# Layer 0's last norm: half blocks, the mean subtracted by TensorE, Ln and Exp in place of root and reciprocal, norm and gate fused on VectorE

## The chip, the cores and the metric

The kernel runs on one core of a Trainium2 chip, in one launch. The metric is the device time of a run in microseconds (us): the median of three runs of the kernel before is 10,872.56 us (10,855.62 to 10,873.84). All data are float32.

## The reference, cut to what matters

The kernel computes a network of four layers. Layer 0 is a selective scan over four images of 64 x 64 tokens with 256 inner channels, and it ends in a norm over the channels, a gate and a projection back to 128 channels:

```python
y = ys[:, 0]... + ys[:, 1]... + ys[:, 2]... + ys[:, 3]...   # four scan directions
mu = jnp.mean(y, axis=-1, keepdims=True)
var = jnp.mean(jnp.square(y - mu), axis=-1, keepdims=True)
y = (y - mu) * jax.lax.rsqrt(var + LN_EPS) * ln_w + ln_b
y = y * jax.nn.silu(z)
return y @ w_out
```

The result is added to the layer's input, and layer 1 reads the sum. Layers 1 to 3 and their feed-forward parts are not touched by the change.

## The kernel before, in words

**Where the work stands.** `layer0` runs image after image. An image goes through `front` (group norm, input projection), `middle` (convolution, step sizes), the scan, and `back` (the norm above). Channels lie on the 128 partitions, in two halves `h`; tokens lie along the free axis. `back` works on eight blocks of 512 tokens.

**The scan loop** has 512 turns `I`: 4 images x 2 channel halves x 64 chunks of 64 tokens. Turn I of image b is called by its half h and chunk c. Its work comes in two equal parts, kp 0 and kp 1. For each part TensorE makes 32 small products into two PSUM banks (L668; the banks `db` are three), VectorE adds the carry twice (L684) and runs two scans (L687), and GpSimd takes the new carry (L694) and multiplies the states by C in one product of 128 x 2048 elements (L702). Once in a turn, between its two parts, VectorE also multiplies `xo` and `dt` into `du` for the next turn (L644). TensorE sums the states of the turn before last (L722), ScalarE copies these sums out (L736), makes the diagonal tiles of the next turn in half 0 (L636, 16 instructions) and the decay factors (L591).

**What runs beside it.** `front(b + 1)`, `middle(b + 1)` and `back(b - 1)` are generators. The loop takes one step of the running generator at up to three places of a turn:

```python
scan(I, now, 0, bs, st, carry, new)     # two scans
...
    next(beside, None)                  # first place
...
bs = products(now, 1)
if nxt:
    inputs(nxt)                         # L644
scan(I, now, 1, bs, st, carry, new)     # two scans
    next(beside, None)                  # second place
...
if beside and h == 0 and c % 4 == 2:
    next(beside, None)                  # third place
```

So what a step of the first place puts on VectorE stands between the second scan and L644; what a step of the second or third place puts there stands between the fourth scan and the next turn's first. On TensorE, ScalarE and VectorE the order is the written one (`manual_schedule`), and each of them is one queue in order; for GpSimd and for SyncE, which issues the loads and stores, a scheduler sets the order. The order of generators in images 1 and 2 is `back(b - 1)`, `front(b + 1)`, `middle(b + 1)`; in image 3 it is `back(2)` alone; image 0 has other generators there. They begin at chunk 5 of half 0. Whatever is left of them at chunk 59 of half 1 is run at once there, in front of that turn (`if h and c == NCHUNK - QC - 1: for _ in beside: pass`). The beside work has one PSUM bank, `bg`.

`back` has 11 steps a block: loads of `yr`, `zs` and `x` (into tiles `t4k`, four buffers, and `t2k`), a sum of two partial results on GpSimd (L501), the mean over channels by TensorE with a matrix of 1/256 (L508), two subtractions on VectorE (L513), two squares on ScalarE (L517), the variance by TensorE (L521), a root on ScalarE (L523), a reciprocal and two products on VectorE (L525, L527), scale and bias on ScalarE (L530), the product with the gate `zl` on GpSimd (L534), the projection on TensorE (L541), and the residual on VectorE (L545).

**After the loop** the last image's `back(3)` has no loop to run beside. `recurrence_and_attention` runs it beside `prepare(0)`, the first image of layers 1 and 2: one step of `back` for every two of `prepare`, with two banks in turn (`bg`, `blk`). Here a scheduler sets the order on every engine. `prepare(0)` must be done before the attention loop (its first score product is L1431).

Below stand the functions that the diff touches and their callers, with the profile's line numbers.

Of the kernel before, what the change touches and what calls it, by code (L numbers as in the profile page):

```python
# [8 lines left out]
AF = mybir.ActivationFunctionType  # L9
ALU = mybir.AluOpType  # L10
# [4 lines left out]
P = 128  # L15
# [4 lines left out]
D = 128  # L20
BLK = 512
# [3 lines left out]
DI = 256  # L25
# [34 lines left out]
def tl(pool, shape, tag, dtype=F32, bufs=None):  # L60
    return pool.tile(shape, dtype, name=tag, tag=tag, bufs=bufs)
# [99 lines left out]
def layer0(cm, x, W, x1, also, kept):  # L161
# [5 lines left out]
    with ExitStack() as ctx:  # L167
# [30 lines left out]
        nc.vector.tensor_scalar(A, A, -1.0, None, ALU.mult)  # L198
        d4 = tl(wp, [P, 2], "d4")
        nc.vector.tensor_scalar(d4, vec[:, 2, :], 4.0, None, ALU.mult)  # L200
        avg = tl(wl, [P, P], "avg")
        nc.vector.memset(avg, 1.0 / DI)

        mask = tl(wp, [P, QR], "mask")
        for r in range(4):
# [277 lines left out]
        def back(b, bank, tmp=tmp, t4=t4):  # L483


            def fetched(k, *names):
# [2 lines left out]
                    nc.sync.dma_start(t, img[b][name][:, :, k * BLK : (k + 1) * BLK])  # L489
                return ts  # L490

            (y0,) = fetched(0, "y0")
            yield
            for k in range(NBLK):
                cols = slice(k * BLK, (k + 1) * BLK)
                xr = tokens(b, k, tmp)
                y, zl = fetched(k, "yr", "zs")
                yield
                yield
                yield  # L500
                nc.gpsimd.tensor_tensor(y, y, y0, ALU.add)  # L501
                if k + 1 < NBLK:
                    (y0,) = fetched(k + 1, "y0")
                yield
                yield
                ps = bank()
                for h in range(2):
                    nc.tensor.matmul(  # L508
                        ps, lhsT=avg, rhs=y[:, h, :], start=(h == 0), stop=(h == 1)
                    )  # L510
                sq = []
                for h in range(2):
                    nc.vector.tensor_tensor(y[:, h, :], y[:, h, :], ps, ALU.subtract)  # L513
                yield
                for h in range(2):
                    sq.append(tl(tmp, [P, BLK], "t2k"))
# [6 lines left out]
                nc.scalar.activation(sd, ps, AF.Sqrt, bias=cm.eps5[:, 0:1])  # L523
                yield
                nc.vector.reciprocal(ps, sd)  # L525
                for h in range(2):
                    nc.vector.tensor_tensor(y[:, h, :], y[:, h, :], ps, ALU.mult)  # L527
                yield
                for h in range(2):
                    nc.scalar.activation(  # L530
                        y[:, h, :], y[:, h, :], AF.Identity,
                        bias=vec[:, 4, h : h + 1], scale=vec[:, 3, h : h + 1],
                    )
                nc.gpsimd.tensor_tensor(y, y, zl, ALU.mult)  # L534
                yield
                yield
                ps = bank()
                po = ps.rearrange("p (t c) -> p t c", c=D)
                for i in range(4):
                    for h in range(2):  # L540
                        nc.tensor.matmul(  # L541
                            po[:, i, :], lhsT=y[:, h, i * P : (i + 1) * P], rhs=w_out[:, h, :],
                            start=(h == 0), stop=(h == 1),
                        )
                nc.vector.tensor_tensor(xr, xr, po, ALU.add)  # L545
                nc.sync.dma_start(x1[b, cols, :].rearrange("(t p) c -> p t c", p=P), xr)


# [1808 lines left out]
```

## Time and profile before

| | |
|---|---|
| median of three runs | 10,872.56 us |
| the profiled execution's own time | 10,860.27 us |
| its span, first to last instruction | 10,858.5 us |
| VectorE (DVE) busy | 7,823.8 us, 72% of the span |
| TensorE (PE) busy | 8,928.9 us, 82% |
| ScalarE (ACT) busy | 5,313.2 us, 49% |
| GpSimd (POOL) busy | 5,452.4 us, 50% |
| scan loop, first to last scan | 341 to 6,246 us |
| from there to the first score product L1431 | 6,246 to 6,640 us |

The profile is one execution. A group row names the line, the engine, the operation, its output and inputs, their shapes (partitions x elements) and the count; behind the bar stand the time in which at least one of them ran, the mean time of one in ns, and the idle time of the engine just before them with what ended most of it. A matmul in float32 leaves two records. TensorE's records overlap, so that the time of a group, and not its count by its mean, tells how long TensorE was taken.

### The profile page before, as it was taken

Reading aid. Unit: us, or ns where it says so; the run is one execution under the profiler, and the core shown is the slowest. Engines: PE = TensorE matmul, PEld = TensorE weight load, DVE = VectorE, ACT = ScalarE, POOL = GpSimd, SP = SyncE. Lnnn points to the kernel's source line nnn. Section 1 sums busy time; section 2 is a strip of 40 time slices with the busy share of each in tenths; the row PEclk is TensorE's granted clock in tenths of the full one; section 3 lists DMA queues with packets and bytes.
Section 4 is the critical chain, followed back from the end, with each engine's and each line's share of the span. In section 5 each row is a group of like instructions: output and inputs, shape, how many; then the busy total and the mean of one; then the engine's idle time right before and its main releaser. Section 6 shows DMA issues by size and latency. Waiting matters only on the chain. (4 is left out here: it accounts for less than half of the span.)

```text
span 10858.5 us, 190052 instructions
## 1 busy us (share of the span) xinstructions
PE 8928.9 (82%) x72040; PEld 4226.5 (39%) x72040; DVE 7823.8 (72%) x10667; ACT 5313.2 (49%) x13151; POOL 5452.4 (50%) x2661
## 2 busy tenths in 40 slices
PE   6668998779887788887788846999999956998886
PEld 2333443334333333333333323444444434544442
DVE  1799999999999999999999965546361132445546
ACT  5557554556444565445532124767676613333321
POOL 0579999879888888888899920000000000000000
PEclk7789998889888889888888968999999976577767
DMA  5434554335443345443333231111100083012101
GB/s 150 105 91 128 145 140 110 103 98 153 131 119 110 109 117 141 130 119 102 99 94 94 74 117 38 36 35 36 32 27 16 16 226 70 26 37 57 41 20 47
DMA packets 1155618, 960.91 MB, mean 88 GB/s; under 512 B 191940, under 2 KB 905384, under 8 KB 1148312
## 3 DMA queue, kind: packets, MB, share of 16 engines
q1 hardware_dynamic: 1140888, 898.41, 29.2%
q0 software_dynamic: 13824, 50.34, 2.6%
q8 instruction: 579, 9.49, 0.4%
q14 instruction: 327, 2.68, 0.1%
HBM read 616.68 MB, written 331.61 MB: 87 GB/s over the span
## 5 line engine op out<-in xcount | busy, mean ns | idle before, releaser
L687 DVE TENSOR_TENSOR_SCAN big<-dA,db 128x1024 f32<-128x1024 f32 x2048 | 4679.5, 2286 | 81.9 <-PE db L668 3.1
L702 POOL TENSOR_TENSOR big<-big,ct 128x2048 f32<-128x2048 f32 x1024 | 4648.2, 4539 | 78.7 <-DVE big L687 0.2
L668 PE MATMUL db<-dg,du 32*64 32x256 f32 x32768 | 1952.0, 427 | 822.1 <-DVE db L684 674.5
L722 PE MATMUL yp<-big,both 128*64 128x256 f32 x16384 | 2368.9, 438 | 66.2 <-ACT yc L736 58.2
L722 PEld LDWEIGHTS yp<-big,both 128*64 128x64 f32 x16384 | 1250.6, 155 | 1152.0 <-issue 752.8
L668 PEld LDWEIGHTS db<-dg,du 32*64 32x64 f32 x32768 | 672.3, 138 | 2079.6 <-issue 1909.5
L736 ACT COPY yr<-yp 128x64 f32<-128x64 f32 x1024 | 224.4, 220 | 1618.2 <-PE yp L722 1617.8
L1480 PE MATMUL av<-e,x 128*128 128x512 f32 x2048 | 974.0, 592 | 4.6 <-ACT e L1475 4.6
L1431 PE MATMUL qk<-a,xT 128*128 128x512 f32 x2048 | 966.6, 594 | 8.7 <-ACT e L1435 7.9
L1435 ACT ACTIVATE e<-qk,nk 128x512 f32<-128x512 f32 x1024 | 693.3, 685 | 539.5 <-PE qk L1431 538.4
L591 ACT ACTIVATE dA<-dp,A 128x252 f32<-128x252 f32 x2048 | 866.1, 499 | 98.1 <-DVE big L687 48.3
L636 ACT ACTIVATE dg<-mask,BT 128x32 f32<-128x32 f32 x4096 | 898.5, 323 | 5.3 <-PE db L668 5.3
L1010 POOL TENSOR_TENSOR g_rs<-g_rs,qrow 128x4 f32<-128x4 f32 x32 | 41.1, 1285 | 1500.4 <-DVE g_rs L1009 1500.4
L694 POOL TENSOR_TENSOR cy<-big,a 128x32 f32<-128x32 f32 x1008 | 347.4, 345 | 571.3 <-DVE big L687 374.8
L1431 PEld LDWEIGHTS qk<-a,xT 128*128 128x128 f32 x2048 | 378.0, 190 | 462.4 <-issue 358.0
L1480 PEld LDWEIGHTS av<-e,x 128*128 128x128 f32 x2048 | 381.6, 190 | 434.8 <-issue 393.7
L1475 ACT ACTIVATE e<-e 128x1024 f32<-128x1024 f32 x510 | 538.8, 1056 | 15.5
L644 DVE TENSOR_TENSOR du<-xo,dt 128x256 f32<-128x256 f32 x512 | 533.1, 1041 | 12.8 <-DMA xo<-xT_d 12.8
L1956 ACT ACTIVATE e<-s 72x576 f32<-72x576 f32 x448 | 273.3, 643 | 512.2 <-PE s L1949 509.2
L1967 POOL COPY vp<-vt 72x160 f32<-72x160 f32 x56 | 19.6, 352 | 909.6 <-PE po L1973 906.8
L2189 DVE SCALAR_TENSOR_TENSOR tex<-x,gw,tex 128x128 f32<-128x128 f32 x768 | 264.2, 344 | 254.6 <-PE x L2183 239.8
L1913 DVE TENSOR_REDUCE mx<-s 96x6 f32<-96x864 f32 x224 | 226.0, 1047 | 291.0 <-PE s L1905 290.7
(528 smaller groups left out, 9883.4 us busy)
## 6 DMA issues: line engine op xcount, KB each, us to landing
ct<-ct_d SPq DMA_DIRECT2D x1024, 128.0 KB
xo<-xT_d SPq DMA_DIRECT2D x2048, 32.0 KB
dg_d<-dg SPq DMA_DIRECT2D x256, 256.0 KB
dg<-dg_d SPq DMA_DIRECT2D x256, 256.0 KB
t4k<-xc_d SPq DMA_DIRECT2D x384, 132.0 KB
dT_d<-t2k SPq DMA_DIRECT2D x256, 128.0 KB
dp<-dl_d SPq DMA_DIRECT2D x256, 128.0 KB
dt<-dT_d SPq DMA_DIRECT2D x512, 64.0 KB
```

Source lines behind the costliest of these rows:

```text
L591: nc.scalar.activation(w["dA"][:, :, g, n, 1:], w["dp"][:, g, :, 1:], AF.Exp, scale=A[:, w["h"], g, n : n + 1],)
L636: nc.scalar.activation(q["dg"][:, n, :], mask, AF.Copy, scale=BT[:, q["c"], n : n + 1])
L644: nc.vector.tensor_tensor(q["du"], q["xo"], q["dt"].unsqueeze(1).to_broadcast([P, 2, P]), ALU.mult)
L668: nc.tensor.matmul(bs[j][p * TC : (p + 1) * TC, g * NH0 : (g + 1) * NH0, t0 : t0 + QR], lhsT=q["du"][rows, kp, g * TC : (g + 1) * TC], rhs ...
L687: nc.vector.tensor_tensor_scan(st[:, u].rearrange("p n t -> p (n t)"), q["w"]["dA"][:, c % QC].rearrange("p g n t -> p (g n t)"), bs[j].re ...
L694: nc.gpsimd.tensor_tensor(new[:, us, :], st[:, us, :, TC - 1], quads[(I + 1) // QC]["a0"][:, (c + 1) % QC] .rearrange("p g n -> p (g n)"). ...
L702: nc.gpsimd.tensor_tensor(sv, sv, q["ct"].rearrange("p n t -> p (n t)").unsqueeze(1) .to_broadcast([P, 4, NH0 * TC]), ALU.mult,)
L722: nc.tensor.matmul(yp[p * TC : (p + 1) * TC], lhsT=both, rhs=st[:, :, p * NH0 + n, :], start=(n == 0), stop=(n == NH0 - 1),)
L1431: nc.tensor.matmul(ps, lhsT=me["xT"][:, kt * P : (kt + 1) * P], rhs=me["a"][k], start=True, stop=True,)
L1435: nc.scalar.activation(e[:, j, :], ps, AF.Exp, bias=me["nk"][:, kt : kt + 1], scale=2.0)
L1475: nc.scalar.activation(es[g + 2], es[g + 2], AF.Exp)
L1480: nc.tensor.matmul(avs[b, k], lhsT=img[b]["x"][:, kt, :], rhs=e[:, j, :], start=(kt == 0), stop=(kt == NT - 1),)
```

## The change

`back` now works on half blocks of 256 tokens, two for each block. For each:

- TensorE takes y less its mean in one bank, with a matrix `cen` (identity less 1/256) and a matrix `navg` (-1/256): four products of 256 columns. ScalarE copies the result out (`yc`) and squares it (`sq`).
- TensorE makes the negative variance with `navg`; ScalarE takes Ln of the variance plus 1e-5 and Exp of -0.5 times it, into the same bank.
- VectorE has two fused instructions for each channel half: (yc x ln_w) x root into PSUM, and (that + ln_b) x zl into `yc`.
- TensorE projects 256 tokens, and VectorE adds them to the residual.

GpSimd's gate product is gone; its sum y + y0 stays. A block has 12 steps in place of 11.

```diff
-        avg = tl(wl, [P, P], "avg")
-        nc.vector.memset(avg, 1.0 / DI)
+        navg = tl(wl, [P, P], "navg")
+        nc.vector.memset(navg, -1.0 / DI)
+        cen = tl(wl, [P, P], "cen")
+        nc.vector.tensor_tensor(cen, cm.ident, navg, ALU.add)
...
-                yield
-                ps = bank()
-                for h in range(2):
-                    nc.tensor.matmul(
-                        ps, lhsT=avg, rhs=y[:, h, :], start=(h == 0), stop=(h == 1)
-                    )
-                sq = []
-                for h in range(2):
-                    nc.vector.tensor_tensor(y[:, h, :], y[:, h, :], ps, ALU.subtract)
-                yield
-                for h in range(2):
-                    sq.append(tl(tmp, [P, BLK], "t2k"))
-                    nc.scalar.activation(sq[h], y[:, h, :], AF.Square)
-                yield
-                ps = bank()
-                for h in range(2):
-                    nc.tensor.matmul(ps, lhsT=avg, rhs=sq[h], start=(h == 0), stop=(h == 1))
-                sd = tl(tmp, [P, BLK], "t2k")
-                nc.scalar.activation(sd, ps, AF.Sqrt, bias=cm.eps5[:, 0:1])
-                yield
-                nc.vector.reciprocal(ps, sd)
-                for h in range(2):
-                    nc.vector.tensor_tensor(y[:, h, :], y[:, h, :], ps, ALU.mult)
-                yield
-                for h in range(2):
-                    nc.scalar.activation(
-                        y[:, h, :], y[:, h, :], AF.Identity,
-                        bias=vec[:, 4, h : h + 1], scale=vec[:, 3, h : h + 1],
-                    )
-                nc.gpsimd.tensor_tensor(y, y, zl, ALU.mult)
-                yield
-                yield
-                ...
-                nc.vector.tensor_tensor(xr, xr, po, ALU.add)
+                for s in range(2):
+                    part = slice(s * half, (s + 1) * half)
+                    yield
+                    ps = bank().rearrange("p (h t) -> p h t", h=2)
+                    for o in range(2):
+                        for h in range(2):
+                            nc.tensor.matmul(
+                                ps[:, o, :], lhsT=cen if o == h else navg, rhs=y[:, h, part],
+                                start=(h == 0), stop=(h == 1),
+                            )
+                    yc = tl(tmp, [P, 2, half], "t2k")
+                    sq = tl(tmp, [P, 2, half], "t2k")
+                    nc.scalar.copy(yc, ps)
+                    nc.scalar.activation(sq, ps, AF.Square)
+                    yield
+                    ps = bank().rearrange("p (h t) -> p h t", h=2)
+                    for h in range(2):
+                        nc.tensor.matmul(
+                            ps[:, 0, :], lhsT=navg, rhs=sq[:, h, :],
+                            start=(h == 0), stop=(h == 1),
+                        )
+                    nc.scalar.activation(
+                        sq[:, 0, :], ps[:, 0, :], AF.Ln, bias=cm.eps5[:, 0:1], scale=-1.0
+                    )
+                    nc.scalar.activation(ps[:, 0, :], sq[:, 0, :], AF.Exp, scale=-0.5)
+                    yield
+                    for h in range(2):
+                        nc.vector.scalar_tensor_tensor(
+                            ps[:, 1, :], yc[:, h, :], vec[:, 3, h : h + 1], ps[:, 0, :],
+                            ALU.mult, ALU.mult,
+                        )
+                        nc.vector.scalar_tensor_tensor(
+                            yc[:, h, :], ps[:, 1, :], vec[:, 4, h : h + 1], zl[:, h, part],
+                            ALU.add, ALU.mult,
+                        )
+                    yield
+                    ps = bank()
+                    po = ps[:, 0:half].rearrange("p (t c) -> p t c", c=D)
+                    for i in range(2):
+                        for h in range(2):
+                            nc.tensor.matmul(
+                                po[:, i, :], lhsT=yc[:, h, i * P : (i + 1) * P],
+                                rhs=w_out[:, h, :], start=(h == 0), stop=(h == 1),
+                            )
+                    nc.vector.tensor_tensor(
+                        xr[:, 2 * s : 2 * s + 2, :], xr[:, 2 * s : 2 * s + 2, :], po, ALU.add
+                    )
```

More of the change, by code (lines that the diff above doesn't have):

```diff
@@ L490, in fetched @@
                 return ts
+            half = BLK // 2
             (y0,) = fetched(0, "y0")
@@ L529, in back @@
-                for h in range(2):
-                    nc.scalar.activation(
-                        y[:, h, :], y[:, h, :], AF.Identity,
-                        bias=vec[:, 4, h : h + 1], scale=vec[:, 3, h : h + 1],
-                    )
-                nc.gpsimd.tensor_tensor(y, y, zl, ALU.mult)
-                yield
-                yield
-                ps = bank()
-                po = ps.rearrange("p (t c) -> p t c", c=D)
-                for i in range(4):
+                for s in range(2):
[14 more added lines that the diff above has]
+                    ps = bank().rearrange("p (h t) -> p h t", h=2)
@@ L540, in back @@
                     for h in range(2):
                         nc.tensor.matmul(
-                            po[:, i, :], lhsT=y[:, h, i * P : (i + 1) * P], rhs=w_out[:, h, :],
+                            ps[:, 0, :], lhsT=navg, rhs=sq[:, h, :],
                             start=(h == 0), stop=(h == 1),
                         )
-                nc.vector.tensor_tensor(xr, xr, po, ALU.add)
+                    nc.scalar.activation(
+                        sq[:, 0, :], ps[:, 0, :], AF.Ln, bias=cm.eps5[:, 0:1], scale=-1.0
+                    )
```

## The prediction

> **What bounds the kernel now.** First the page, because `back` lives in the scan loop and in the stretch behind it. Its slices (40 of 271 us, busy share in tenths) and two of its groups:
>
> ```profile
> DVE  1799999999999999999999965546361132445546
> POOL 0579999879888888888899920000000000000000
> ...
> L687 DVE TENSOR_TENSOR_SCAN big<-dA,db 128x1024 f32<-128x1024 f32 x2048 | 4679.5, 2286 | 81.9 <-PE db L668 3.1
> L702 POOL TENSOR_TENSOR big<-big,ct 128x2048 f32<-128x2048 f32 x1024 | 4648.2, 4539 | 78.7 <-DVE big L687 0.2
> ```
>
> VectorE is full from 340 to 6,246 us, and GpSimd nearly: a turn has 4 scans of 2.29 on one and 2 products of 4.54 on the other. From the starts of L687 in the timeline, a turn with nothing beside it takes 10.1 to 10.2 us. So inside the loop what is put on VectorE costs its time, or more. Where it costs more, the instructions of `du` show:
>
> ```profile
> L644 DVE TENSOR_TENSOR du<-xo,dt x512: 359/512/4772, 338.2 to 6230.5; 128x256 f32<-128x256 f32 x171
> ```
>
> The same instruction takes 0.36 or 4.77 us. Two answers of the timeline (start, us, engine) say when, in image 3:
>
> ```profile
> 4962.28 0.40 DVE L644 TENSOR_TENSOR du<-xo,dt 128x256 f32<-128x256 f32 x1
> ...
> 5023.73 0.69 DVE L545 TENSOR_TENSOR t2k<-t2k,bg 128x512 f32<-128x512 f32 x1
> 5024.34 4.72 DVE L644 TENSOR_TENSOR du<-xo,dt 128x256 f32<-128x256 f32 x1
> ...
> 5024.26 4.52 POOL L702 TENSOR_TENSOR big<-big,ct 128x2048 f32<-128x2048 f32 x1
> ```
>
> The reader is to see that L644 straight after the scan takes 0.40; behind 0.69 us of beside work it begins 0.08 us after GpSimd's product and ends 0.28 us after it. Both read two SBUF tensors, and one waits for the other. L702 begins 0.42 us (GpSimd idle) to 0.6 us after the scan's end; L644s that began 0.10 us or more ahead of it took at most 0.53 us. So a step of the first place that holds VectorE longer than about 0.4 us costs some 5 us whatever it does, and one of the second place costs its own time. Turns in image 3's `back` bear it out: first place with L545 15.2, with L525/L527 15.2, with L513 15.2 and 15.7 (and 14.3 and 11.6 where GpSimd was late); second place with L545 10.5, with L513 11.2, with L525/L527 14.5.
>
> The work to be replaced, in the loop (24 of 32 blocks):
>
> ```profile
> L525 DVE RECIPROCAL bg<-t2k 128x512 f32<-128x512 f32 x24 | 80.0, 3333 | 0.0
> L534 POOL TENSOR_TENSOR t4k<-t4k 128x1024 f32<-128x1024 f32 x24 | 56.3, 2346 | 10.4 <-ACT t4k L530 10.4
> L448 ACT ACT_TABLE_LOAD x50 | 64.2, 1283 | 0.9
> L523 ACT ACT_TABLE_LOAD x24 | 30.8, 1283 | 0.4
> ```
>
> and the waits behind the loop (6,255 to 6,640 us), where the sum's two waits are the only large ones that `back` brings to VectorE:
>
> ```profile
> DVE t2k L545 <- PE bg L541: 12.5, 3, 6.1
> ...
> DVE t2k L545 <- PE blk L541: 9.3, 3, 6.3
> ```
>
> **The parts.** *VectorE's own time.* Before, a block has 3.34 (L525) + 4 x 0.68 (L513, L527) + 0.68 (L545) = 6.7 us. After, it has 8 fused instructions and 2 additions on 256 columns. The addition: L644 alone, 0.40. The fused one is bounded by 0.41 (L450, the same form on 512 without a pointer, 0.67 less 256 columns at 1.04 ns) and 0.48 (L2063, with a pointer, 0.75, likewise); I take 0.48, the same kind. So a group S of four is 1.9 us, and a block 4.7: 2.0 us less. All have a PSUM operand, and L527, which has one too, stays at 0.67 to 0.69 under GpSimd's products.
>
> *Where they fall.* The order of the two built programs gives each step's place. Per image, before: L525/L527 3 in first places and 5 later, L513 4 and 4, L545 4 and 4. Measured against 10.15 us a turn, the turns of `back` (chunks 7 to 44) cost 102, 100 and 92 us: 98 per image. After, with 4 VectorE steps a block in place of 3: S 7 in first places, 9 later; additions 6 in first places, 10 later. Per image:
>
> - S first: 7 x 4.65 (turns of `middle` with 2.1 us there, L450 to L454, take 14.8) = 32.6. S later: 9 x 1.9 = 17.1.
> - Additions first: 0.40 us leaves L644 about 0.17 us ahead of L702, so no wait: 6 x 0.45 = 2.7; later, 7 x 0.35 = 2.5 (3 more are in the next item).
> - Third places. A TensorE step that needs VectorE's second-place step of its own turn holds back the next products, 1.95 us: `front` shows it, 19.2 us at chunk 46 (three L296) against 15.4 at 45 (two). The projection after S, 3 times: 1.1 (half of L541's 2.2 a block) + 1.95 = 3.1 each, 9.3. The centring after an addition, 3 times: 2.2 (as many columns as L508's 2.1 a block) + 1.95 = 4.2, 12.6.
> - TensorE elsewhere: the centring that waits for the one bank until a first-place addition, 3 x 1.5 = 4.5 (BT's copy L429 in that place costs 1.2 with a shorter product behind it); ten other centrings of 2.2 in a half turn that has some 1.7 to spare: before, L521 of the same size cost 1.0 to 2.5 at chunks 8 and 13; 1.2 each, 12; two variances in third places, 2.4.
> - GpSimd: L534 hid under L525 (turns with it: 10.4 to 10.5), so its going gives nothing. Two of the sums L501 (2.4) now stand in turns without a collision and delay L644: 4.8.
>
> The sum is 100.5, against 98: +7 for three images. VectorE's saving is eaten by one more step in the wrong place and by third-place waits.
>
> At those chunks the granted clock was 0.54 (4,994 to 5,001 us) after TensorE had been idle for 2.07 us. The Trainium skill (TensorE: Matmul & The Clock Gate, Part 1) has the clock fall after an idle window of about 3.4 us; by it those centrings would run at full clock and cost nearer 0.6, 6 us less an image. The row decides.
>
> *ScalarE.* Per half: copy and square 1.2, Ln and Exp 0.8, and tables. L448 is Ln, and the page of the loop shows a load before each one, 1.28 us; the built program has 62 loads for 64 Ln and 64 for 64 Exp at the new lines, against 28 before roots, and 28 fewer elsewhere: 70 more in all, 90 us of ScalarE. In the loop that hides: a turn of half 0 holds 3.5 (L636) + 1.7 (L591) + 0.6 (L736), and `front`'s turns, with two loads and more work, take 10.1.
>
> *`middle` comes 8 steps later.* `back` of images 1 and 2 has 8 more steps, and the steps left at chunk 59 are run in one piece. Before, nothing with VectorE work is left; after, the last block's nine steps are (L429 to L475; in the built order seven VectorE instructions stand behind chunk 58). They form one chain through one bank: w_dt 1.44, ScalarE 4.6 and 5.9 (with one and two loads), VectorE 2.05, for both halves, with an overlap of 0.7 each: 16.5; then 2 x (0.8 + 0.6 + 1.2 + 0.6) + hops = 6.8; less the last copy, plus the products: TensorE can give the next scan its data about 25 us late. In its old places this cost 11.5 (chunks 55 to 58). 2 x 13.5 = +27. `front` keeps its cost, about 27 an image.
>
> *Behind the loop* (8 blocks). Less VectorE time 8 x 2.0 = 16; less collision with L534 (five slow instructions there have 10 us over their usual time, 5.9 under L534) 6; the waits of L545 (21.8) and L513 (3.2) 25: -47. But a half block is now a chain: projection 1.7, centring 2.8, ScalarE 1.2, variance 1.4 (sizes of this stretch, where L541 and L508 are slower), Ln, load, Exp 2.2, hops 0.4: 9.7 us from one S to the next, because the bank is freed by S. In the built order VectorE has 2 to 11 us of other work between them; summed over 15 gaps the lacking time is 45. So -2. The Trainium skill (ScalarE: Activation LUTs, Table sets: the hidden batching unit) says that one set holds Ln and Exp, one load for both; then the chain is 8.4 and the sum some 17 us lower. Loads before each in the built program speak against it; I go by them.
>
> **Sum.** 7 + 27 - 2 = +32 on the profiled execution's 10,860.3 (span 10,858.5 and 1.8 around it): 10,892. The median of runs is 12 us above that execution: 10,905.
>
> **Rivals.** *The lock is missed (faster).* Where GpSimd is late, L644 passes: at chunk 35 of half 1 in image 1, L450 to L454 stood in the first place and the turn took 13.3, L644 0.40. If S (1.9 us) ended ahead of L702, 21 places would cost 2.0 in place of 4.65: -56, 10,849. It needs GpSimd to be 1.5 us behind at that point; the sum L501 does that in few turns, and L534's going makes it rarer. *The chain behind the loop is hidden (no change).* VectorE's other work covers the 45 us: 10,860. It decides at 9.7 us against the 6 us that the built order leaves on average. *The additions meet the lock (much slower).* 0.17 us of margin is small; if they miss it, 18 x 4.2 = +76: 10,981. *The tables are one set:* 10,888 and no further.
>
> **Numbers.** The forecast 0.50, with its own range of 10,870 to 10,945; missed lock 0.17; hidden chain (or a flush that overlaps more) 0.20; additions in the lock 0.13. A measurement of this kernel tells 0.2%, 22 us, from no change. Faster: the missed lock and a little of the hidden chain, 0.18. Same: most of the hidden chain and the low end of the forecast, 0.27. Slower: the rest, 0.55. The range reaches from 10,842 to 10,985.
>
> **What would show it.** L644's spread: about 7 of some 4.7 us in each `back`, under S, and none under the additions; turns at chunks 10, 14, 26, 30, 42, 46 long by third-place waits; a gap of about 25 us at chunk 59 of half 1 in images 1 and 2, and none in image 3; 126 loads at the new lines, 1.28 each; behind the loop S waiting for ScalarE, and L1431 near 390 us after the last scan. The forecast is wrong if the first-place S costs 2 us, if additions cost 5, if chunk 59 stays at 10 us, or if L1431 comes 30 us sooner after the last scan.

## The result, and the profile after

The changed kernel takes 10,947.22 us (median of 6 runs, 10,910.27 to 10,957.58), the kernel before in the same comparison 10,874.51 us (6 runs): a ratio of 1.0057, with a 95% interval of 1.0037 to 1.0076. It is slower by 73 us between the medians, and by 40 to 83 us by the interval. The profiled execution took 10,950.13 us, its span is 10,948.4 us.

The page of the changed kernel, with the rows that answer to those of before. Lines behind `back` have moved by 9: the scan is L696, `du` L653, GpSimd's product L711, the carry's addition L693. The slices are the busy shares in tenths; in a row, busy time and mean of one in ns stand behind the first bar, and the idle time before it with what ended it behind the second.

```profile
DVE  1699999999998999989999956545451132445546
POOL 0579999779878888878899910000000000000000
...
L696 DVE TENSOR_TENSOR_SCAN big<-dA,db 128x1024 f32<-128x1024 f32 x2048 | 4679.3, 2286 | 82.0 <-PE db L677 3.1
L711 POOL TENSOR_TENSOR big<-big,ct 128x2048 f32<-128x2048 f32 x1024 | 4646.1, 4537 | 79.3 <-POOL cy L703 0.4
```

The scans and the products cost what they did. VectorE, full before, now shows slices of 8: it has less to do in the loop and waits more. Its new groups in the changed kernel, and the loads of tables in front of Ln and Exp:

```profile
L535 DVE SCALAR_TENSOR_TENSOR bg<-t2k,vec,bg 128x256 f32<-128x256 f32 x112 | 53.3, 476 | 24.5 <-ACT bg L532 22.7
L539 DVE SCALAR_TENSOR_TENSOR t2k<-bg,vec,t4k 128x256 f32<-128x256 f32 x112 | 54.1, 483 | 3.5
L552 DVE TENSOR_TENSOR t2k<-t2k,bg 128x256 f32<-128x256 f32 x56 | 22.5, 402 | 23.4 <-PE bg L548 23.4
...
L532 ACT ACT_TABLE_LOAD x64 | 82.1, 1283 | 1.2
L529 ACT ACT_TABLE_LOAD x62 | 79.5, 1283 | 35.7 <-PE bg L525 23.7 <-PE blk L525 11.4 <-issue 0.2
```

The instructions cost what the forecast gave them: the fused ones 0.48 us, the additions 0.40. The time must have gone elsewhere. Adding up the turns from the starts of the scans gives where (us; half 1 of image 3 is 653.7 and 653.4):

| | before | after | difference |
|---|---|---|---|
| start to first scan | 341.4 | 349.3 | +7.9 |
| image 0 | 1,443.4 | 1,446.7 | +3.3 |
| half 0 of images 1, 2, 3 (`back`, then `front`) | 2,327.1 | 2,333.9 | +6.8 |
| half 1 of images 1, 2 (`middle`) | 1,479.9 | 1,528.8 | +48.9 |
| last scan to first score product | 394.9 | 408.0 | +13.1 |
| from there to the end | 4,218.1 | 4,228.2 | +10.1 |

The first and the last row hold code that the change doesn't touch; over all profiled executions of this study they lie between 341.4 and 350.9, and between 4,199.8 and 4,231.3. So 18 of the 90 us between the two profiled executions are such scatter, and 72 lie in the loop and behind it: two thirds of them in half 1 of two images, where not one instruction was changed. In half 0 the turns of `back` (chunks 7 to 48, over 10.15 us a turn) cost 104.2, 103.6 and 96.5 us against 102.0, 100.2 and 91.7 before (chunks 7 to 44): +10.4. That is one pair of executions. Two later runs with the old `back` in the same places (`before_shift`, `old_loop_new_tail`) have sums of 287 and 286 us for the three images, where this pair has 294; two with the new one (`after_noflush`, `after_tail3`) have 301 and 312, where it has 304. The means are 17 us apart.

Three places of the changed kernel show the mechanisms. First, VectorE's timeline in a turn with S, the four fused instructions of L535 and L539, in its first place (start, duration in us, engine, line):

```profile
5133.53 0.46 DVE L535 SCALAR_TENSOR_TENSOR bg<-t2k,vec,bg 128x256 f32<-128x256 f32 x1
...
5135.47 3.44 DVE L653 TENSOR_TENSOR du<-xo,dt 128x256 f32<-128x256 f32 x1
...
5143.64 0.40 DVE L552 TENSOR_TENSOR t2k<-t2k,bg 128x256 f32<-128x256 f32 x1
5143.95 0.17 DVE L693 TENSOR_TENSOR db<-db,cy 128x16 f32<-128x16 f32 x1
```

and GpSimd's in the same stretch:

```profile
5134.10 4.52 POOL L711 TENSOR_TENSOR big<-big,ct 128x2048 f32<-128x2048 f32 x1
```

L653 began inside GpSimd's product and ended 0.29 us behind it, at 5138.91. This happens under 7 S in each image (in chunks 14, 19, 21, 30, 35, 37 and 46 of all three, 3.4 us mostly), and under no addition that stands alone in a first place: there L653 takes 0.42. (At chunk 48 of images 1 and 2 it takes 3.1 behind an addition, but the first step of `front`, with 0.70 us of VectorE work, stands between them.)

Second, TensorE in chunk 14 of the same image, where an addition stands in the second place and a centring (L514, the products that take y less its mean) in the third (in brackets the idle time before the instruction, and what ended it):

```profile
5077.84 1.22 PE L514 MATMUL bg<-t4k,cen 128*128 128x256 f32 x2 [3.78 <-DVE t2k L552]
5078.86 1.91 PE L514 MATMUL bg<-t4k,navg 128*128 128x256 f32 x4
5080.56 1.06 PE L514 MATMUL bg<-t4k,cen 128*128 128x256 f32 x2
5081.56 1.16 PE L677 MATMUL db<-dg,du 32*64 32x256 f32 x16
```

TensorE, in order, holds the centring until the addition has freed the bank, and the next turn's products stand behind it. VectorE's next carry addition, L693, then waited 6.18 us for them.

Third, VectorE at chunk 59 of half 1 in image 1, where the rest of `middle` is run in one piece:

```profile
3261.06 2.29 DVE L696 TENSOR_TENSOR_SCAN big<-dA,db 128x1024 f32<-128x1024 f32 x1
3263.26 0.27 DVE L431 COPY BT<-bg 128x128 f32<-128x128 f32 x1
3269.54 0.70 DVE L452 SCALAR_TENSOR_TENSOR bg<-bg,t2k 128x512 f32<-128x512 f32 x1 [6.01 <-ACT t2k L450]
...
3279.72 0.70 DVE L452 SCALAR_TENSOR_TENSOR bg<-bg,t2k 128x512 f32<-128x512 f32 x1 [8.03 <-ACT t2k L450]
...
3292.37 0.18 DVE L693 TENSOR_TENSOR db<-db,cy 128x16 f32<-128x16 f32 x1 [10.49 <-PE db L677]
```

29 us pass between two scans. Images 1 and 2 both have this (turns of 39.1 and 40.1 us), image 3 does not.

### The profile page after: what moved, and what is told of

Read it like the earlier page. It is cut to its first block, busy times and chain, and to the rows that moved or that the text cites. A ratio compares the mean times of both kernels' runs of the same rounds, so it can differ in the third digit from the quotient of the medians.

```text
span 10948.4 us, 191237 instructions
## 1 busy us (share of the span) xinstructions
PE 9006.6 (82%) x72552; PEld 4357.2 (40%) x72552; DVE 7758.5 (71%) x10796; ACT 5414.1 (49%) x13317; POOL 5359.3 (49%) x2629
## 5 line engine op out<-in xcount | busy, mean ns | idle before, releaser
L696 DVE TENSOR_TENSOR_SCAN big<-dA,db 128x1024 f32<-128x1024 f32 x2048 | 4679.3, 2286 | 82.0 <-PE db L677 3.1
L711 POOL TENSOR_TENSOR big<-big,ct 128x2048 f32<-128x2048 f32 x1024 | 4646.1, 4537 | 79.3 <-POOL cy L703 0.4
L677 PE MATMUL db<-dg,du 32*64 32x256 f32 x32768 | 1913.7, 421 | 649.2 <-DVE db L693 499.9
L731 PE MATMUL yp<-big,both 128*64 128x256 f32 x16384 | 2340.8, 434 | 71.3 <-ACT yc L745 58.6
L1444 ACT ACTIVATE e<-qk,nk 128x512 f32<-128x512 f32 x1024 | 692.9, 685 | 540.2 <-PE qk L1440 539.4
L1484 ACT ACTIVATE e<-e 128x1024 f32<-128x1024 f32 x510 | 538.7, 1056 | 15.3
L653 DVE TENSOR_TENSOR du<-xo,dt 128x256 f32<-128x256 f32 x512 | 525.1, 1026 | 12.8 <-DMA xo<-xT_d 12.8
L693 DVE TENSOR_TENSOR db<-db,cy 128x16 f32<-128x16 f32 x2016 | 333.2, 165 | 189.5 <-PE db L677 169.5
```

The source lines that it names most:

```text
L653: nc.vector.tensor_tensor(q["du"], q["xo"], q["dt"].unsqueeze(1).to_broadcast([P, 2, P]), ALU.mult)
L677: nc.tensor.matmul(bs[j][p * TC : (p + 1) * TC, g * NH0 : (g + 1) * NH0, t0 : t0 + QR], lhsT=q["du"][rows, kp, g * TC : (g + 1) * TC], rhs ...
L696: nc.vector.tensor_tensor_scan(st[:, u].rearrange("p n t -> p (n t)"), q["w"]["dA"][:, c % QC].rearrange("p g n t -> p (g n t)"), bs[j].re ...
L711: nc.gpsimd.tensor_tensor(sv, sv, q["ct"].rearrange("p n t -> p (n t)").unsqueeze(1) .to_broadcast([P, 4, NH0 * TC]), ALU.mult,)
L731: nc.tensor.matmul(yp[p * TC : (p + 1) * TC], lhsT=both, rhs=st[:, :, p * NH0 + n, :], start=(n == 0), stop=(n == NH0 - 1),)
L1444: nc.scalar.activation(e[:, j, :], ps, AF.Exp, bias=me["nk"][:, kt : kt + 1], scale=2.0)
```

## The experiments

### The flush at chunk 59

The changed kernel itself ran in the result's comparison only. Each run below is timed beside the kernel before, and its ratio to it is what can be compared.

Theory: +49 in half 1 come from `middle`'s last steps being run in one piece, and from nothing in the new `back` itself. `after_noflush` is the changed kernel with the eight steps given back:

```diff
             # front, second loop over blocks
-                yield
+                if b < 2:
+                    yield
```

> The changed kernel, but `front` of images 2 and 3 ends eight of its steps one call later, so that `middle` stands again where it stood before and nothing of it is left at chunk 59. If the flush at chunk 59 costs what the trace shows (half 1 of images 1 and 2 longer by 24.9 and 24.1 us), the time falls by about 49 us, from 10,947 to 10,898. If the loss lies in the greater work of TensorE and ScalarE, or in the run, it stays at 10,947.

Measured: 10,899.87 us, ratio to before 1.0053 (1.0037 to 1.0069). The figure of 10,898 was met, but beside a kernel before that was 17 us lower than in the result's comparison; the ratio was 1.0057 there, so the time does not show the gain. The trace does: half 1 of images 1 and 2 fell from 762.8 to 742.8 and from 766.0 to 743.0, by 43, close to the 49; half 0, where `front` now comes in other places, rose by 6.3 and 2.5. The other side of it, `before_8steps`, is the kernel before made late by eight empty steps:

```diff
+                            iter([None] * (8 if b else 0)),
                             front(b + 1, own_bank), wait(I - c + NCHUNK),
```

> The kernel before, with eight empty steps ahead of `front` in images 1 and 2: `back` as it was, only `middle` and `front` come 8 steps later. Flush theory: +49 us, 10,874 to 10,923, with a turn of some 39 us at chunk 59 of half 1 in both images. If the flush costs only together with the new `back`, no change.

Measured: 10,883.86 us, 1.0034 (1.0018 to 1.0051). Half 1 rose by 24.0 in each image, to 761.9 and 766.0, just the changed kernel's values. So the flush is shown from both sides, 20 to 24 us an image. What was not expected: half 0 fell by 19.5 and 10.2, without any work taken away (two later runs with the same half 0 as the kernel before lie up to 5.5 and 5.3 us below it; the fall goes beyond that by 14 and 5). Only the places of `front`'s steps had changed. That led to the experiments on places.

### What a place costs

Theory: a step of VectorE work costs by the place it falls in (S in a first place some 5 us, in a second one 2.1, an addition in a first one next to nothing), and a third place costs TensorE's wait. Without third places, a block of 12 steps falls in two places a turn, so all S of an image stand in the same kind of place, and one empty step in front chooses which. In the last image nothing else depends on it:

```diff
-                if beside and h == 0 and c % 4 == 2:
+                if beside and h == 0 and c % 4 == 2 and b < B - 1:
                     next(beside, None)
```

> Edit: the changed kernel, but in the last image `back` gets no third place. A block has 12 steps and a turn two places, so every fused group S now falls in a first place and every addition in a second one. Output unchanged. Theory (the price goes by the place: S first 5.1 us, S second 2.1, addition first 0.4, and a third place behind S or an addition costs 3 to 7 us by TensorE's wait): half 0 of image 3 has 16 x 5.1 = 82 plus 16 x 0.3 for the additions plus some 5 for the sums, about 90 us over 10.15 us a turn, against 96.5 in the changed kernel: about the same, since six dear third places go and nine S become dearer. Rival (the steps cost what they hold VectorE for, and the long turns come from `back`'s work as such): about 16 x 2.3 = 37 plus the third places, and no difference to the other parity.

> Edit: as the one with every S in a first place, with one empty step ahead of `back` in the last image, so that every S falls in a second place and every addition in a first one. Output unchanged. Theory (price by place): 16 x 2.1 + 16 x 0.4 + 5 = about 45 us over 10.15 us a turn in half 0 of image 3, against 96.5 in the changed kernel: the turn periods fall by about 50 us, the time to about 10,897. Rival (third places cost nothing to speak of and S costs the same wherever): no more than 10 us less. Rival (additions in first places meet GpSimd's product once all of them stand there): 16 x 4.7, and nothing is gained.

The second has this in addition:

```diff
+                    if b == B - 1:
+                        gens.insert(0, iter([None]))
                     beside = run(*gens)
```

Half 0 of image 3 took 761.3 us in the changed kernel, 761.5 with every S in a first place, and 721.2 with every S in a second one. By time: 10,910.03 (one run) and 10,892.02 (1.0025 to before, interval 1.0013 to 1.0036). The groups of VectorE over chunks 7 to 54 of that image, first of the changed kernel:

```profile
L653 DVE TENSOR_TENSOR du<-xo,dt 128x256 f32<-128x256 f32 x48 | 51.6, 1075 | 0.0
L693 DVE TENSOR_TENSOR db<-db,cy 128x16 f32<-128x16 f32 x192 | 31.9, 166 | 30.0 <-PE db L677 29.6 <-POOL cy L703 0.3
```

then with S in first places:

```profile
L653 DVE TENSOR_TENSOR du<-xo,dt 128x256 f32<-128x256 f32 x48 | 75.7, 1576 | 0.1
L693 DVE TENSOR_TENSOR db<-db,cy 128x16 f32<-128x16 f32 x191 | 31.8, 166 | 13.0 <-PE db L677 9.9 <-POOL cy L703 3.1
```

and with S in second places:

```profile
L653 DVE TENSOR_TENSOR du<-xo,dt 128x256 f32<-128x256 f32 x48 | 34.5, 719 | 0.0
L693 DVE TENSOR_TENSOR db<-db,cy 128x16 f32<-128x16 f32 x192 | 32.1, 167 | 13.7 <-PE db L677 12.6 <-POOL cy L703 0.7
```

The same 48 instructions of `du` take 51.6, 75.7 or 34.5 us. Without third places the wait for TensorE's products falls from 29.6 to some 10 to 13 us. In the first variant the two cancel, as its expectation said. In the second both gains are kept: 17 us of `du`, 17 of the products' wait, 6 of L552's wait for L548. What is left there, 57.7 us over 10.15 a turn (45 were expected), is mostly the work itself: 30.7 for S and 6.3 for the additions. The fear that additions meet GpSimd's product when all stand in first places is refuted: all 16 of L653 behind one took 0.42.

If the price belongs to the place and not to the work, it must hold for `middle` in the kernel before too. There its VectorE steps fall in first places in images 1 and 2, and in second places beside image 0, whose half 1 is 48 and 52 us shorter. `before_shift`:

```diff
                             front(b + 1, own_bank), wait(I - c + NCHUNK),
+                            iter([None] * (1 if b else 0)),
                             middle(b + 1, own_bank, t4, "t4k", 2),
```

> Edit: the kernel before with one empty step ahead of `middle` in images 1 and 2, so that its VectorE steps (L429 to L454), which stand in first places there, fall in second places, as `middle(1)` beside image 0 does already (half 1 of image 0: 689.8 us against 737.9 and 742.0). Output unchanged. Theory (the price goes by the place, for whatever work): half 1 of images 1 and 2 falls to some 690 to 700, 45 each, and the time to about 10,780; then the good places of the best kernel owe some 75 of what they bring to `middle`, which the change does not touch. Rival (half 1 of image 0 is shorter for another reason, the first image's own): no more than 10 us.

Measured: 10,761.94 us, 0.9906 (0.9890 to 0.9923). Half 1 went from 737.9 to 692.9 and from 742.0 to 690.6. `du` over chunks 5 to 58 of half 1 in image 1, in the kernel before:

```profile
L644 DVE TENSOR_TENSOR du<-xo,dt 128x256 f32<-128x256 f32 x54 | 61.9, 1146 | 0.0
```

and in `before_shift`:

```profile
L644 DVE TENSOR_TENSOR du<-xo,dt 128x256 f32<-128x256 f32 x54 | 26.1, 483 | 0.0
```

36 of the 45 us show at this one instruction. One empty step in each of two images brings 100 us; the whole change takes 65 us of work from VectorE (7,823.8 to 7,758.5 us busy).

### Moving `du` out of the way

Theory: the whole price of a first place is `du` meeting GpSimd's product. Then it goes when `du` stands ahead of the first place, in either kernel:

```diff
                 scan(I, now, 0, bs, st, carry, new)
+                if nxt:
+                    inputs(nxt)
...
                 bs = products(now, 1)
-                if nxt:
-                    inputs(nxt)
```

> The kernel before, with the product L644 (du) moved ahead of the first place, straight behind the second scan. Lock theory: L644 then always starts ahead of GpSimd's product, its 512 records sum to about 210 us in place of 533, and first-place steps cost their own time: about 280 us less (200 to 330), 10,590. If first-place steps are dear because TensorE comes late, and the lock only shows it, less than 60 us.

> The changed kernel with the same move. Lock theory: each of the 21 first-place groups S costs 2.0 in place of 5.1 us, and the moved lines of `middle` and `front` gain as in the kernel before: about 240 us less than the changed kernel, 10,700, and some 110 above the kernel before with the same move, since third-place waits, the flush and the stretch behind the loop are untouched. If the lock is what makes the change lose, the two moved kernels are within 20 us of each other.

Measured: 10,783.34 (0.9940, 0.9921 to 0.9960) for the kernel before, a gain of 74 where 280 were expected; 10,858.18 (0.9996, 0.9984 to 1.0007) for the changed one, some 66 less by the ratios (1.0057 to 0.9996) where 240 were expected. The difference of 75 between the two stays: the changed kernel's loss does not hang on `du`. The theory of the price is half refuted. `du` fell from 533.1 to 371.9 us in the kernel before, but a turn of `middle` still took 13 to 15 us, and half 1 of images 1 and 2 gained next to nothing (738.5 and 736.9, after 737.9 and 742.0). VectorE's timeline in such a turn of `before_du`:

```profile
2776.00 0.45 DVE L644 TENSOR_TENSOR du<-xo,dt 128x256 f32<-128x256 f32 x1
2776.38 0.28 DVE L429 COPY BT<-bg 128x128 f32<-128x128 f32 x1
...
2784.38 0.18 DVE L684 TENSOR_TENSOR db<-db,cy 128x16 f32<-128x16 f32 x1 [2.91 <-PE db L668]
```

and TensorE's:

```profile
2770.34 1.95 PE L722 MATMUL yp<-big,both 128*64 128x256 f32 x16
...
2776.71 1.92 PE L436 MATMUL bg<-t2k,w_dt 8*128 8x512 f32 x2 [1.43 <-DVE BT L429]
2778.56 3.68 PE L722 MATMUL yp<-big,both 128*64 128x256 f32 x16
2782.18 1.16 PE L668 MATMUL db<-dg,du 32*64 32x256 f32 x16
```

`du` takes 0.45 here, but TensorE waits for VectorE's first-place copy L429 before it can use `bg`; the sums L722 and the products L668 stand behind that, and VectorE waits 2.91 us for the products. Over the execution this wait of L684 for L668 rose from 114.3 to 177.0 us. Most of the 2.91 us, 1.73, goes with TensorE's clock: behind the 1.43 us of idle time the 16 sums L722 take 3.68 where they took 1.95 ahead of it. The two stretches, with times in us (length, busy time of PE, weight loads, VectorE, ScalarE and GpSimd), then the granted clock as a share of the full one, DMA share and GB/s:

```profile
2770.00:2776.70 6.70, 5.18 (x96) 2.75 (x80) 6.56 (x8) 1.70 (x4) 6.54 (x5) 1.00 0.23 61
2776.70:2783.40 6.70, 6.62 (x34) 2.40 (x34) 4.70 (x4) 4.67 (x10) 6.25 (x3) 0.52 0.36 89
```

Two waits lay over each other under a first place, and removing one left the other. No run gave the beside work a second bank, so what the shared bank alone costs is not shown.

### The stretch behind the loop

`old_loop_new_tail` has the old `back` in the loop and the new one for the last image only:

```diff
-                    gens = [back(b - 1, own_bank) if b else also(
+                    gens = [back_old(b - 1, own_bank) if b else also(
```

> Edit: the kernel before inside the scan loop, the changed `back` only behind the loop for the last image. Output unchanged. The first score product should come 408 us after the last scan as in the changed kernel, 13 us later than before, with S waiting for ScalarE by about 40 us there; the loop stays at 5,904. Theory (the chain behind the loop costs 13): about 10,882. The forecast's term (-2): 10,867. Rival (the later score product in the changed kernel came from the flush and the later turns ahead of it): 10,869, first score product at 395.

The first score product came 405.2 us after the last scan, 10.3 later than in the kernel before, at a loop of 5,900.7. In the four profiled kernels with the old `back` behind the loop it came at 392.1 to 398.6, in the six with the new one at the same pace at 405.2 to 408.2, `after_noln` below left out. By time it is 10,867.65 beside 10,860.35, 1.0014 (1.0001 to 1.0027), an interval that begins almost at nothing. So the 10 us are read from the trace; the time alone would not settle them. `after_tail3` lets more work stand between two steps of `back`:

```diff
-                if i % 2:
+                if i % 3 == 2:
                     next(rest, None)
```

> Edit: the changed kernel, with one step of `back(3)` for every three of `prepare(0)` behind the loop, in place of one for every two. Output unchanged. Theory (the chain of a half block, 9.7 us, is too long for the work that stands between two S): with half as much again between them the waits of S for ScalarE, 39.8 us, fall under 15, and the first score product comes 10 to 20 us sooner, 390 to 398 us after the last scan; the time falls by as much, to about 10,932. Rival (ScalarE or TensorE bounds this stretch, and S's waits only show it): the waits of S fall, others take their place, and the score product stays at 408 or comes later because the end of `back` now stands behind `prepare`.

Measured: 10,897.02, 1.0039 (1.0021 to 1.0056), with the first score product at 375.4, 32.6 sooner. The waits of VectorE behind the loop (us in total, times, the longest), first of the changed kernel:

```profile
DVE bg L535 <- ACT bg L532: 22.7, 8, 3.9
DVE blk L535 <- ACT blk L532: 17.1, 7, 4.2
...
DVE de L1149 <- ACT z L1177: 12.8, 4, 4.3
...
DVE xT L1325 <- PE qk L1014: 10.4, 5, 3.0
```

and of `after_tail3`:

```profile
DVE bg L535 <- ACT bg L532: 15.3, 6, 3.6
...
DVE blk L535 <- ACT blk L532: 11.9, 5, 4.2
```

S's waits fell from 39.8 to 27.2, not under 15, yet the gain is more than twice what that gives. The rest is `prepare`'s own: all of VectorE's waits in the stretch fell from 154.3 to 122.5 us, among them those of L1149 (12.8 to 7.4) and L1325 (10.4 to 5.4). With fewer steps of `back` pressed in between, the chain of `prepare`, which sets the end, is held up less. The last addition of `back` now ends 311 us after the last scan and not 281, still ahead of the score product.

`after_noln` replaces Ln by a square, which needs no table of its own; the root is then not what is computed. It was to show the price of the loads of Ln:

```diff
-                        sq[:, 0, :], ps[:, 0, :], AF.Ln, bias=cm.eps5[:, 0:1], scale=-1.0
+                        sq[:, 0, :], ps[:, 0, :], AF.Square
```

> Edit: the changed kernel with a square (no table of its own, no bias) in place of the logarithm, so that ScalarE loads one table per half block and not two; the variance's root is then not what is computed. It shows what the 64 loads of Ln cost. Theory: in the loop ScalarE's loads are hidden, so it stays at 5,963 within 10; behind the loop the chain of a half block is 1.3 shorter and 15 gaps give some 17: first score product at 391. Rival (ScalarE's load holds up the loop too, through the diagonal tiles or the decay factors): half 0 of images 1 to 3 falls by more than 5 each, without the third-place turns being shorter. Rival (S behind the loop waits for TensorE's products and not for ScalarE): 405 or later.

The edit took away more than the loads of Ln. Its trace has no load at L529, and at L532, the line of Exp, two are left of 64:

```profile
L532 ACT ACT_TABLE_LOAD x2 | 2.6, 1283 | 0.0
```

So 124 loads are gone and not 62, 28 of them behind the loop. The loop stayed (5,955.8 against 5,962.8; half 0 of image 3 at 761.3 in both, its long turns too), and the first score product came at 381.9, 26 sooner. The loads of both functions are hidden in the loop and cost some 26 us behind it. The 17 expected stood for those of Ln alone, which no run shows. S's waits behind the loop are still 20.3 us without either. Its one run took 10,913.38 us.

### All good places together

`best1` is the changed kernel with what the experiments taught: a block of 10 steps (two empty ones less), no third place for `back`, one empty step in front, and the slower pace behind the loop.

```diff
             (y0,) = fetched(0, "y0")
             yield
+            yield
...
                 y, zl = fetched(k, "yr", "zs")
                 yield
                 yield
-                yield
                 nc.gpsimd.tensor_tensor(y, y, y0, ALU.add)
                 if k + 1 < NBLK:
                     (y0,) = fetched(k + 1, "y0")
-                yield
                 for s in range(2):
...
-                if beside and h == 0 and c % 4 == 2:
+                if beside and h == 0 and c % 4 == 2 and (not b or c > 45):
```

> Edit: the changed kernel, but a block of `back` takes 10 steps (two empty ones left out), `back` gets no third place and begins with one empty step, so that in all images every S falls in a second place and every addition in a first one, and `middle` ends in its turns with nothing left at chunk 59; behind the loop one step of `back(3)` for every three of `prepare(0)`. Output unchanged. Theory (price by place, flush, chain, each as measured alone): half 0 of images 1 to 3 falls by 40 each, half 1 of images 1 and 2 by 22 each, the first score product comes 33 sooner: 197 in all, about 10,750. Rival (the centring now stands one step behind GpSimd's sum, and TensorE waits for it in front of the next products): 24 blocks x 2 us, some 50 are lost again, 10,800.

> Edit: as the one before, with `du` (L653) moved ahead of the first place, right behind the first two scans. Output unchanged. Theory: what stays in first places of `front` and `middle` no longer meets GpSimd's product through `du`; alone the move brought 65 us of the loop in the kernel before, of which half 0 of images 1 and 2 (24 and 25) had `back` in first places, so here 40 remain: about 10,710. Rival (all that it brought was `back`'s first places, which are gone): 10,745.

`best1` took 10,680.64 us, 0.9828 (0.9812 to 0.9845); `best2`, with `du` moved as above, 10,671.69, 0.9819 (0.9802 to 0.9835). Both beat the kernel before by 1.7 to 1.8%. Half 0 of images 1 to 3 fell by 38, 42 and 37 against the changed kernel, as forecast. Half 1 fell by 62 and 65 and not by 22: the shift also put `middle` into second places, which wasn't planned (45 of it, as `before_shift` then showed), although a smaller flush remains (turns of 23.0 at its place). Behind the loop only 7 of the 33 us came: with two empty steps less, S follows S sooner, and its waits there are 37.5 us again. Moving `du` is worth 15 us of loop here by the traces (9 by the medians, with intervals that overlap), nearer to the rival's nothing than to the 40 expected: what it would gain has gone with the first places.

The old `back` was not tried with its work in chosen places, so whether the new one is the better in good places is open.

## Why the prediction was right or wrong

The forecast was a small loss, +32, with 10,905 us in a range to 10,945; it came to +73, at 10,947. The direction is right, and each mechanism that it named is in the trace. The terms of the flush and of the stretch behind the loop were short, and the term of `back` came out nearly right by luck.

**`back` in the loop, +7 forecast, +10.4 measured.** (The second figure is of the one pair; the means above give +17.) The seven S of first places per image are there, and cost 5.1 each (turns of 15.2 to 15.3 without a third place, two of twelve 16.5) where 4.65 were put. The third places were too cheap: chunks 10, 26 and 42 took 16.6 where the forecast's terms give 15.2, and chunks 14, 30 and 46 took 20.3 to 21.6 where they give 19.0. The ten other centrings, put at 12 an image, cost 2 to 4 (their turns over 10.15). About 9 us too much and 10 too little an image nearly cancel, which is luck. The forecast's list of turns before was also the low end in one kind: the five second places with L525/L527 in image 3 took 14.5, 14.6, 15.7, 16.8 and 15.7, and not 14.5.

**TensorE's clock is behind them.** In the changed kernel's loop 30 of the 48 centrings follow TensorE's other work at once, and 29 of these took 1.99 us. The nine of chunks 14, 30 and 46, behind 3.7 to 5.4 us of idle time, took 3.4 to 3.8. The nine of chunks 9, 25 and 41, which wait 1.17 us for the bank behind an addition, took 1.99 three times, in turns of 10.7, and 3.5 to 3.7 six times, in turns of 12.3 (0.45 + 1.5 were put for both). The projections of chunks 10, 26 and 42 took 2.08 behind 5.9 us of idle time; those of other chunks behind 0.92 us took 1.16. Stretches of the changed kernel with their clock (columns as above): such a projection, the centring shown above, the gap at chunk 59, and the turns behind that gap:

```profile
5026.30:5030.80 4.50, 4.29 (x42) 2.48 (x42) 0.43 (x2) 1.57 (x4) 3.40 (x3) 0.50 0.02 6
...
5077.80:5081.60 3.80, 3.76 (x15) 2.57 (x15) 0.00 (x0) 0.00 (x0) 3.72 (x2) 0.50 0.00 0
...
3263.40:3292.40 29.00, 11.83 (x50) 3.99 (x52) 4.33 (x8) 13.86 (x19) 6.43 (x5) 0.53 0.36 93
3292.40:3320.00 27.60, 23.51 (x264) 10.82 (x260) 27.16 (x25) 7.44 (x28) 21.86 (x10) 0.88 0.28 81
```

The forecast put the low clock in the wrong turns. In its own row of 0.54 the variance L521, with as many columns as a centring, took 3.78 in the kernel before:

```profile
4993.90 2.39 PE L668 MATMUL db<-dg,du 32*64 32x256 f32 x24 [2.07 <-DVE db L684]
4996.22 3.78 PE L521 MATMUL bg<-t2k,avg 128*128 128x512 f32 x4
```

It laid the cost of such turns on the ten centrings that stand elsewhere, and these ran at 1.99. To the third places, where TensorE had waited, it gave 2.2 for a centring and 1.1 for a projection, which are near the times without idle time. It did not carry the low clock on to the flush either.

By the Trainium skill (TensorE: Matmul & The Clock Gate, Part 1) the clock falls after an idle window of about 3.4 us. Chunks 14, 30 and 46 fit it, and so do the ten centrings, which the forecast's estimate by that page had at the full clock. The six long centrings behind 1.17 us, if only the idle time right before them counts, do not; why three of the nine stayed at 1.99 is open.

**The flush, +27 forecast, +49 measured.** This is the term that was mis-sized, by 11 an image. The turn grew by 29 to 30 us where 25 were put, and the forecast's own list shows why: in the gap TensorE runs at a clock of 0.53, so w_dt for the second half took 2.07 and not 1.44, the two turning products 2.07 each and not 1.2, the transposes 1.11 and not 0.8. That is 0.6 + 1.7 + 0.6, some 3 of the 4 to 5 us. (Its 16.5 for both halves are 16.1 by its own terms.) The larger part is the credit: 11.5 was taken back for the turns that the flush empties, but the rest of half 1 was only 4 and 6 us shorter than before (762.8 less 29.1 against 737.9; 766.0 less 30.1 against 742.0). A part of that: in image 1 two first-place turns of the kernel before had been cheap (13.1 and 13.3), and all of the changed kernel's take 14.8 to 15.3.

**ScalarE's tables.** There are 126 loads at the new lines, 1.28 us each; the 96 in the loop are hidden, as `after_noln` shows. The choice against one set for Ln and Exp (the Trainium skill, ScalarE: Activation LUTs, Table sets: the hidden batching unit) holds for this program: 62 loads at Ln, 64 at Exp. Going without nearly all of both was worth 26 us behind the loop.

**Behind the loop, -2 forecast, +10 to +13 measured.** Three of the parts hold: VectorE's busy time in the stretch fell from 270.9 to 250.8 (20, where 22 were put), the waits of L545 and L513 are gone, and S waits 39.8 where 45 were put. What the sum lacked is a wait at the additions, 8.4 (L552 for L548), and some 11 more in waits of `prepare` beside it: all of VectorE's waits in the stretch rose from 121.5 to 154.3. `after_tail3` shows that `prepare`'s waits can move; which of them the new `back` brought is open.

**`front` keeps its cost.** Right in sum: less what `back` takes, half 0 of images 1 and 2 moved by -6.7 and +2.0, no more than the scatter. As a rule it is wrong, since `before_8steps` moved it by 10 to 20 with its places alone.

**The rivals.** The lock was missed in single turns only: with S in first places throughout, `du` took 0.41 once in 16. The additions did not meet it. The hidden chain is refuted by the 39.8 us that S waits. The one set of tables is refuted by the 126 loads.

**The lock itself** was half of the reason. Under a first place there are two waits, `du` for GpSimd and TensorE's one bank for VectorE, the second made longer by TensorE's lower clock behind it, as the runs with `du` moved show; the forecast's 4.65 a turn was near the measured 5.1 because it came from whole turns, which hold both.

## What to carry to other kernels

Where work is threaded step by step into fixed places of a loop, the number of steps is part of the kernel: eight more of them in each of two images cost 49 us, by the trace, in a piece of code that was not edited, and a single empty one in each gained 100. Before counting what an edit saves on an engine, list which step falls in which place, and choose steps per block so that the heavy ones fall where nobody waits. When a slow place has been explained by one wait, move that wait away on its own: if the turn stays long, another one lay under it. And when TensorE has waited, look at the granted clock before giving its next products the times they have elsewhere.

## What the runs showed of the hardware that was not expected

- TensorE's clock halves more easily than expected: the same eight products of 256 columns took 1.99 or 3.5 to 3.7 us behind 1.17 us of idle time; the clock was 0.52 behind 1.43 us of it in `before_du`, where it had been 1.00, and 0.53 over a gap of 29 us in which TensorE worked 11.8.
- `du`, a VectorE instruction on two SBUF tensors, waits for GpSimd's product (0.40 to 4.7 us), while the fused ones, with one operand or their result in PSUM, ran at 0.46 to 0.49 in the same product: the S at 5133.53 overlaps the product from 5134.10 without a loss.
- The start of the kernel and its last 4,200 us, with the same code in all, differ by up to 9.5 and 31.5 us between executions; a difference of some 20 us in the time alone says little about a change here.
